# Layer 0 of a four-layer convolution stack: the last 1x1 convolution ordered by channel groups in place of chunks

## The chip, the core and the metric

The kernel runs on one core of one Trainium2 chip. Its engines work side by side, each through its own list of instructions in order: TensorE (PE; its weight loads are shown apart as PEld), VectorE (DVE), ScalarE (ACT), GpSimd (POOL) and SyncE (SP), which issues transfers. The metric is the device time of the whole kernel in microseconds (us), as the median of several runs.

## The reference, cut to what matters

The input x has 4 images of 64 channels and 256 x 256 pixels, all float32. Four residual layers follow one another. The change touches layer 0 alone, and in it the last line, the 1x1 convolution from 192 channels to 64, and the addition of x.

```python
def reference(x, L0_conv_w_in, L0_conv_w_dw, L0_conv_fft_filter, L0_conv_w_out, ...):
    # layer 0
    x = x + _L0_conv_ref(_gn(x), L0_conv_w_in, L0_conv_w_dw, L0_conv_fft_filter, L0_conv_w_out)
    # layers 1, 2 and 3 follow, each x = x + layer(_gn(x), ...); they are not touched
    ...
    return x

def _L0_conv_ref(x, w_in, w_dw, fft_filter, w_out):
    x = jnp.einsum('bchw,oc->bohw', x, w_in)                     # 64 -> 384 channels
    B, C, H, W = x.shape
    xp = x.reshape(B, C, H // 8, 8, W // 8, 8).transpose(0, 1, 2, 4, 3, 5)
    xf = jnp.fft.rfft2(xp) * fft_filter                          # a filter on 8x8 patches
    xp = jnp.fft.irfft2(xf, s=(8, 8))
    x = xp.transpose(0, 1, 2, 4, 3, 5).reshape(B, C, H, W)
    x = lax.conv_general_dilated(x, w_dw, ..., padding=[(1, 1), (1, 1)], feature_group_count=C)
    x1, x2 = jnp.split(x, 2, axis=1)
    x = jax.nn.gelu(x1, approximate=False) * x2                  # 192 channels
    return jnp.einsum('bchw,oc->bohw', x, w_out)                 # the last 1x1 conv: 192 -> 64
```

## The kernel before

Layer 0 works in 128 steps (4 images, 32 strips of 8 rows each); a loop turn `t` has several strips in hand at different stages: it transforms strip t+2, expands and inverts strip t+1, does the depthwise convolution of strip t, and the last 1x1 convolution (`project`) and the residual of strip t-1. Everything that TensorE writes goes to PSUM, in pairs of banks that are handed out in turn from four buffers:

```python
def pair(name):

    return pp.tile([128, 2, 512], F32, tag=f"p{next(turn) % 4}", name=name)

halves = [slice(0, C), slice(C, 128)]                                # C = 64
quarters = [slice(k * Q, (k + 1) * Q) for k in range(4)]             # Q = 32
```

So the fifth `pair` waits until whoever reads the first has done so. The 192 gated channels of a strip lie in two places. 128 of them are in `h` (partitions: 4 chunks j of two rows each, 32 channels in each; along the free axis 4 channel groups g). The other 64 are in `v` (partitions 0-63 hold the rows of chunks 0 and 1, partitions 64-127 those of chunks 2 and 3, for the gated part). `project(t, m)` does one half m, that is two of the four chunks, into one pair, and `add_residual(t, m)` adds that pair to x, which is in `r`:

```python
def project(t, m):

    chunks = [j for j in (2 * m, 2 * m + 1) if j in chunks_of(t)]
    if not chunks:
        return
    ps = po[t, m] = pair(f"pso_{t}_{m}")
    v, h = vt[t], ht[t]
    for j in chunks:
        for s in range(2):
            nc.tensor.matmul(
                ps[halves[s], j % 2, 0:W].rearrange("p (r w) -> p r w", r=2), woutc[halves[m]],
                v[halves[m], 2 * j : 2 * j + 2, s * HW2 : (s + 1) * HW2],
                start=True, stop=False, tile_position=(m * C, s * C),
            )
    for g in range(4):
        for j in chunks:
            for s in range(2):
                nc.tensor.matmul(
                    ps[halves[s], j % 2, 0:W].rearrange("p (r w) -> p r w", r=2),
                    wout[quarters[j], g, :], h[quarters[j], g, :, s * HW2 : (s + 1) * HW2],
                    start=False, stop=(g == 3), tile_position=(j * Q, s * C),
                )

def add_residual(t, m):
    if (t, m) not in po:
        return
    ps, r = po.pop((t, m)), rt[t]
    for b, row, lo, hi in rows_of(t):
        k = slice(max(lo, 2 * m), min(hi, 2 * m + 2))
        if k.start < k.stop:
            z = slice(k.start - 2 * m, k.stop - 2 * m)
            rk = r[:, k].rearrange("p k r w -> p k (r w)")
            nc.vector.tensor_add(rk, rk, ps[:, z, 0:W])
```

`tile_position` names the place in TensorE's 128 x 128 array that a matmul uses: 64 rows by 64 columns for `woutc` (its operands have 64 partitions each), 32 rows by 64 columns for `wout`. The profile shows each of these float32 matmuls as two LDWEIGHTS and two MATMUL instructions.

The other users of PSUM in a turn are, cut to their matmuls and to what frees the pair:

```python
def transform_x(t):                       # psF: 32 matmuls; ACT copies it to xf
    ...
    nc.scalar.copy(xf[t], ps)

def expand(t, g, k):                      # psu: 4 matmuls; DVE multiplies it by the filter
    ...
    nc.vector.tensor_mul(ups[t, g][:, :, k, :], ps[:, :, 0:384], flt.broadcast_to([128, 2, 384]))

def invert(t, g, i):                      # psy: 32 matmuls; ACT copies it to y, in two parts
    ...

def depthwise(t, i, *transfers):          # psd: 9 taps x 16 matmuls, in tiles of 32 x 32, two pairs
    ...
    tile_position=(q * Q, j * Q),

def vector_tap(t, k):                     # the taps of the third channel group, on DVE (tap 0 on ACT)
    ...
    nc.vector.scalar_tensor_tensor(v, s, wdw[:, 2, k : k + 1], v, ALU.mult, ALU.add)
```

A loop turn, in the order in which each engine gets its instructions (the order of the engines' lists is the order of the code):

```python
for t in range(NS + 2):
    ...
    vector_gelu(t - 1, 0)
    normalize_x(t + 2)
    vector_taps(t, 1)
    vector_gate(t - 1, 0)
    vector_gelu(t - 1, 1)
    vector_taps(t, 2)
    vector_gate(t - 1, 1)
    vector_taps(t, 3, 4)
    if t <= NS:
        loads = [(load_r, t, 0), (load_r, t, 1)]
        if exists(t + 3):
            loads += [(load_x, t + 3, 0), (load_x, t + 3, 1)]
        gate_part(t, depthwise(t, 0, *loads))
    next_stats(t - 1)
    next_norms()

    if exists(t + 2):
        transpose_x(t + 2)
    if exists(t + 1):
        invert(t + 1, 0, 0)
    if t - 1 in rt:
        project(t - 1, 0)
        add_residual(t - 1, 0)
    if exists(t + 2):
        transform_x(t + 2)
    if t - 1 in rt:
        project(t - 1, 1)
    vector_taps(t, 5)
    add_residual(t - 1, 1)
    if exists(t + 1):
        invert(t + 1, 0, 1)
        expand(t + 1, 1, 0)
        expand(t + 1, 1, 1)
        invert(t + 1, 0, 2)
        expand(t + 1, 1, 2)
        expand(t + 1, 1, 3)
    if t - 1 in rt:
        finish(t - 1)                     # statistics of the new rows, on DVE
    ...
    vector_taps(t, 6, 7)
    ...
        d = depthwise(t, 1, *moves)
        vector_taps(t, 8)
        value_part(t, d)                  # DVE multiplies h by psd
    ...                                   # invert(t+1, 1, 2), two expands, invert(t+1, 1, 0), tap 0 of t+1,
                                          # two expands, invert(t+1, 1, 1)
```

Of the kernel before, what the change touches and what calls it, by code (L numbers as in the profile page):

```python
# [17 lines left out]
C = 64  # L18
# [96 lines left out]
class _Net:  # L115
# [113 lines left out]
    def _layer0(self, ctx, dst):  # L229
        tc, nc, a, B, H, W = self.tc, self.nc, self.a, self.B, self.H, self.W  # L230
# [4 lines left out]
        def pair(name):  # L235

            return pp.tile([128, 2, 512], F32, tag=f"p{next(turn) % 4}", name=name)

        small = lambda name: pair(name)[:, 0, :]
        HW2 = W // 2  # L240
        NJ = H // 8
        NS = B * NJ
        Q = 32
        halves = [slice(0, C), slice(C, 128)]
# [11 lines left out]
        with tc.tile_pool(name="l0i", bufs=12) as p_i:  # L256
            bst0 = new_bst0(0)
            for k in range(NJ):
                t = p_i.tile([128, 4, W], F32, tag="st", name=f"st_{k}")
# [12 lines left out]
        ps = small("psf")  # L272
# [11 lines left out]
        woutc = cp.tile([128, C], F32, name="woutc")  # L284
# [14 lines left out]
        x0, xns, xT, xf, ups, yt, lt, vt, ht, rt, po, bst1, gt = ({} for _ in range(13))  # L299

        def load_x(t, *sides, ins=None):
            b, j = place(t)
            if t not in x0:
                x0[t] = p_x.tile([128, 8, HW2], F32, tag="x", name=f"x0_{t}")
            for s in sides:
                d = nc.sync.dma_start(
                    x0[t][halves[s]], a["x"][b, :, 8 * j : 8 * j + 8, s * HW2 : (s + 1) * HW2]
                )
                if ins:
                    self.after(d, ins)  # L310


        def rows_of(t):
            b, j = place(t)
            if j > 0:
                return [(b, 8 * j - 2, 0, 4)]
            parts = [(b - 1, H - 2, 0, 1)] if t > 0 else []
            return parts + ([(b, 0, 1, 4)] if t < NS else [])
# [13 lines left out]
        def normalize_x(t):  # L332
            if not exists(t):
                return

            xn = xns[t] = p_xn.tile([128, HW2 // 16, 2, 8, 8], F32, tag="xn", name=f"xn_{t}")
            self.normalize(
                xn.rearrange("p k n r w -> p r (k n) w"),
                x0.pop(t).rearrange("p r (m w) -> p r m w", w=8), 0, place(t)[0],
            )  # L340
# [33 lines left out]
        def new_y(t):  # L374

            ys = yt[t] = []
            for i in range(3):
                y = p_y.tile([128, 11, W + 2], F32, tag=f"y{i}", name=f"y{i}_{t}")
                nc.gpsimd.memset(y[:, :, 0 : W + 2 : W + 1], 0.0)  # L379
                if place(t)[1] == 0:  # L380
                    nc.gpsimd.memset(y[:, 0:3, 1 : W + 1], 0.0)
                ys.append(y)
# [35 lines left out]
        def chunks_of(t):  # L418
            return range(1) if t == NS else range(4)
# [66 lines left out]
                r = slice(4 * m, 4 * m + g.shape[1])  # L486
                nc.vector.tensor_mul(vt[t][halves[m], r], g[halves[1]], vt[t][halves[1], r])

        def project(t, m):

            chunks = [j for j in (2 * m, 2 * m + 1) if j in chunks_of(t)]
            if not chunks:
                return
            ps = po[t, m] = pair(f"pso_{t}_{m}")
            v, h = vt[t], ht[t]
            for j in chunks:
                for s in range(2):
                    nc.tensor.matmul(  # L498
                        ps[halves[s], j % 2, 0:W].rearrange("p (r w) -> p r w", r=2), woutc[halves[m]],
                        v[halves[m], 2 * j : 2 * j + 2, s * HW2 : (s + 1) * HW2],  # L500
                        start=True, stop=False, tile_position=(m * C, s * C),
                    )
            for g in range(4):
                for j in chunks:
                    for s in range(2):
                        nc.tensor.matmul(  # L506
                            ps[halves[s], j % 2, 0:W].rearrange("p (r w) -> p r w", r=2),
                            wout[quarters[j], g, :], h[quarters[j], g, :, s * HW2 : (s + 1) * HW2],
                            start=False, stop=(g == 3), tile_position=(j * Q, s * C),
                        )  # L510

        def add_residual(t, m):
            if (t, m) not in po:
                return
            ps, r = po.pop((t, m)), rt[t]
            for b, row, lo, hi in rows_of(t):
                k = slice(max(lo, 2 * m), min(hi, 2 * m + 2))
                if k.start < k.stop:
                    z = slice(k.start - 2 * m, k.stop - 2 * m)
                    rk = r[:, k].rearrange("p k r w -> p k (r w)")  # L520
                    nc.vector.tensor_add(rk, rk, ps[:, z, 0:W])  # L521

        def finish(t):
            r = rt[t]
# [67 lines left out]
        with ordered:  # L592

            for t in range(3):
                load_x(t, 0, 1)
            for t in range(2):
                normalize_x(t)
                transpose_x(t)
                transform_x(t)
            for k in range(4):  # L600
                expand(0, 0, k)
            new_y(0)
            for k in range(4):
                expand(0, 1, k)
                if k < 3:
                    invert(0, 0, k)
            for k in range(4):
                expand(1, 0, k)
                if k < 3:
                    invert(0, 1, k)  # L610
            vector_taps(0, 0)

            for t in range(NS + 2):

                if exists(t + 1):
                    new_y(t + 1)
# [19 lines that stand above are left out]
                    invert(t + 1, 0, 0)  # L638
                if t - 1 in rt:
                    project(t - 1, 0)  # L640
                    add_residual(t - 1, 0)
                if exists(t + 2):
                    transform_x(t + 2)
                if t - 1 in rt:
                    project(t - 1, 1)
                vector_taps(t, 5)
                add_residual(t - 1, 1)
                if exists(t + 1):
                    invert(t + 1, 0, 1)
                    expand(t + 1, 1, 0)  # L650
# [5 lines that stand above are left out]
                    finish(t - 1)  # L656
                next_norms()

                if exists(t + 1):
                    copy_y(t + 1)  # L660
                vector_taps(t, 6, 7)
                if t <= NS:
                    moves = [(store, t - 1, 0), (store, t - 1, 1), (load_stats, t, 0), (load_stats, t, 1)]
                    d = depthwise(t, 1, *moves)
                    vector_taps(t, 8)
                    value_part(t, d)
                else:
                    store(t - 1, 0, 1)
                next_norms()

                if t + 1 == NS or place(t + 1)[1] == 0:
                    last_y(t + 1)
                if exists(t + 1):
                    invert(t + 1, 1, 2)
                if exists(t + 2):
                    expand(t + 2, 0, 0)
                    expand(t + 2, 0, 1)
                if exists(t + 1):
                    invert(t + 1, 1, 0)
                vector_taps(t + 1, 0)  # L680
                if exists(t + 2):
                    expand(t + 2, 0, 2)
                    expand(t + 2, 0, 3)
                if exists(t + 1):
                    invert(t + 1, 1, 1)
                next_norms()
                for g in range(2):
                    ups.pop((t + 1, g), None)
                for done, k in ((vt, t - 1), (ht, t - 1), (rt, t - 1), (yt, t - 1), (lt, t - 1)):
                    done.pop(k, None)  # L690
            while norms:
                next_norms()
# [573 lines left out]
```

## Time and profile before

| what | before |
|---|---|
| time, median of 3 runs | 8142.03 us (8135.49 to 8143.44) |
| span of the profiled run | 8139.5 us |
| PE busy | 7787.5 us, 96% |
| DVE busy | 6201.2 us, 76% |
| ACT busy | 3597.8 us, 44% |
| POOL busy | 647.1 us, 8% |
| `project`, wout (L506), PE busy | 503.7 us, 8208 instructions, from 167.2 to 5130.1 us |
| residual addition (L521), DVE busy | 176.1 us, 260 instructions |

The profile is of one execution. A line such as L506 is a line of the kernel before. A group of instructions has its busy time (the union of its instructions), the mean length of one, and the idle time of its engine just before them with whoever ended it. The chain of waits is followed back from the last instruction and tells, for each piece of time, which engine and line everything else hung on. Layer 0 ends at about 5130 us, the other layers take the rest.

### The profile page before, as it was taken

How to read it: one execution, taken by the hardware profiler on the slowest of the kernel's cores; microseconds unless marked ns; L12 is line 12 of the kernel's file. 1: busy time of each engine (PE TensorE's matmuls, PEld its weight loads, DVE VectorE, ACT ScalarE, POOL GpSimd, SP SyncE). 2: the span in 40 equal slices, each digit the busy share in tenths (PEclk: the TensorE clock that was granted, in tenths of full speed). 3: DMA queues.
4: the chain of work that ended last, by engine and by line, in shares of the span. 5: the costliest groups of instructions: out<-in, count | busy, mean ns of one | idle time of the engine just before them, and what ended most of it. 6: DMA issues, size and time to landing. Idle time of an engine off the chain costs nothing.

```text
span 8139.5 us, 402431 instructions
## 1 busy us (share of the span) xinstructions
PE 7787.5 (96%) x191350; PEld 4493.9 (55%) x191350; DVE 6201.2 (76%) x5653; ACT 3597.8 (44%) x3853; POOL 647.1 (8%) x1465
## 2 busy tenths in 40 slices
PE   5999999999999999999999999999998999998887
PEld 3666666666666666666666666333333444443365
DVE  6888888888888888888888888433336998886345
ACT  2444444444444444444444444111115787874111
POOL 0000000000000000000000000000001222221000
PEclk9999999999999999999999999999999999999955
DMA  5222222222222222222111111788885666667779
GB/s 117 58 58 62 59 61 55 55 57 59 60 56 56 57 59 58 58 55 49 42 46 46 43 44 41 187 215 212 222 212 140 176 179 173 172 178 222 257 283 389
DMA packets 520862, 942.83 MB, mean 116 GB/s; under 512 B 44996, under 2 KB 308116, under 8 KB 501812
## 3 DMA queue, kind: packets, MB, share of 16 engines
q1 hardware_dynamic: 438708, 648.59, 29.1%
q0 software_dynamic: 80512, 268.50, 12.0%
q8 instruction: 1500, 24.58, 1.3%
q14 instruction: 142, 1.16, 0.0%
HBM read 648.48 MB, written 268.44 MB: 113 GB/s over the span
## 4 chain that ended last, share of the span: by engine, by line
PE 92%; DMA 4%; DVE 2%; issue 1%; ACT 1%; SPq 0%; ACTq 0%; POOLq 0%; DVEq 0%; POOL 0%
PE psd L434 31%; PE ps L753 12%; PE psy L407 10%; PE psu L369 8%; PE one L936 7%; PE pso L506 6%; PE div L895 5%; DMA x<-x 3%; PE pso L498 3%; PE psF L356 2%; PE psa L1110 2%; PE psz L925 2%; PE psT L346 2%; DMA st<-in_x_dram 1%; PE zero L936 1%
## 5 line engine op out<-in xcount | busy, mean ns | idle before, releaser
L434 PE MATMUL psd<-y,diag 32*32 32x512 f32 x73296 | 2539.8, 597 | 11.3 <-issue 10.8
L472 DVE SCALAR_TENSOR_TENSOR v<-y,sb_w_dw,v 128x2048 f32<-128x2048 f32 x1024 | 2391.9, 2336 | 108.4 <-ACT v L470 86.7
L434 PEld LDWEIGHTS psd<-y,diag 32*32 32x32 f32 x73296 | 1516.7, 103 | 870.0 <-issue 350.5
L414 ACT COPY y<-psy 128x512 f32<-128x512 f32 x1536 | 913.9, 658 | 1782.3 <-PE psy L407 1780.3
L372 DVE TENSOR_TENSOR up<-psu,flt 128x768 f32<-128x768 f32 x1024 | 932.0, 952 | 252.9 <-PE psu L369 252.6
L407 PEld LDWEIGHTS psy<-sb_c_bdft,up 64*64 64x64 f32 x49152 | 834.4, 135 | 335.3 <-issue 170.2
L753 PE MATMUL ps<-xn,wk 64*64 64x512 f32 x9216 | 1003.0, 592 | 9.6 <-ACT xn L210 9.6
L407 PE MATMUL psy<-sb_c_bdft,up 64*64 64x64 f32 x49152 | 901.4, 220 | 14.6 <-issue 13.0
L210 ACT ACTIVATE xn<-x,nb,r 128x1024 f32<-128x1024 f32 (+3 forms) x272 | 487.8, 1796 | 897.6 <-POOL xn L735 810.1
L369 PE MATMUL psu<-win,xf 64*64 64x384 f32 x8192 | 765.1, 485 | 10.5 <-DVE h L454 10.5
L753 PEld LDWEIGHTS ps<-xn,wk 64*64 64x64 f32 x9216 | 340.3, 134 | 664.0 <-issue 663.9
L759 DVE TENSOR_TENSOR xr<-xr,ps 128x512 f32<-128x512 f32 x256 | 173.7, 679 | 658.1 <-PE ps L753 658.1
L881 DVE TENSOR_TENSOR q<-xn 128x2313 f32<-128x2313 f32 (+2 forms) x256 | 627.4, 2494 | 13.1 <-ACT xn L210 13.1
L936 PE MATMUL one<-z,wp 32*32 32x512 f32 x16384 | 593.5, 596 | 15.0 <-issue 13.7
L882 ACT ACTIVATE q<-q 128x2313 f32<-128x2313 f32 (+2 forms) x256 | 528.8, 2085 | 30.0 <-DVE q L881 28.7
L506 PE MATMUL pso<-h,wout 32*64 32x256 f32 x8208 | 503.7, 381 | 0.0
L936 PEld LDWEIGHTS one<-z,wp 32*32 32x32 f32 x16384 | 371.6, 103 | 217.4 <-issue 81.0
L448 ACT ACTIVATE h<-psd 128x1024 f32<-128x1024 f32 x258 | 251.0, 1023 | 530.5 <-PE psd L434 530.5
L895 PE MATMUL div<-q,ones 64*32 64x512 f32 x8192 | 459.5, 593 | 11.6 <-ACT q L882 9.6
L379 POOL MEMSET y<- 128x22 f32 x384 | 52.2, 137 | 4494.6 <-ACT y L387 3478.6
L506 PEld LDWEIGHTS pso<-h,wout 32*64 32x64 f32 x8208 | 287.6, 131 | 197.9 <-issue 99.6
L521 DVE TENSOR_TENSOR r<-r,pso 128x512 f32<-128x512 f32 (+1 forms) x260 | 176.1, 678 | 266.8 <-PE pso L506 266.8
(121 smaller groups left out, 6861.7 us busy)
## 6 DMA issues: line engine op xcount, KB each, us to landing
x<-x SPq DMA_DIRECT2D x240, 640.0 KB, 7.5
x<-x SPq DMA_DIRECT2D x61, 2048.0 KB, 13.5
st<-in_x_dram SPq DMA_DIRECT2D x256, 256.0 KB, 3.6
x<-in_x_dram SPq DMA_DIRECT2D x256, 256.0 KB, 3.8
xr<-x SPq DMA_DIRECT2D x128, 512.0 KB, 5.3
x<-xr POOLq DMA_DIRECT2D x128, 512.0 KB, 6.3
r<-x SPq DMA_DIRECT2D x512, 128.0 KB, 4.1
x<-r POOLq DMA_DIRECT2D x512, 128.0 KB, 3.9
```

The lines of the kernel that those rows point to most:

```text
L369: nc.tensor.matmul(ps[halves[n], s, 0:384], xf[t][halves[s], n, 4 * g + k], win[halves[s]], start=True, stop=True)
L372: nc.vector.tensor_mul(ups[t, g][:, :, k, :], ps[:, :, 0:384], flt.broadcast_to([128, 2, 384]))
L407: nc.tensor.matmul(ps[halves[c], n, s, :, k, :], up[halves[n], s, k, i * 128 + c * C : i * 128 + (c + 1) * C], bdft[halves[n]], start=True ...
L414: nc.scalar.copy(yt[t][i][:, 3:11, w0 : w0 + 64].rearrange("p r (k n w) -> p n r k w", k=4, n=2), ps[:, :, s])
L434: ins = nc.tensor.matmul(d[q // 2][quarters[j], q % 2], diag[quarters[q], i, k, :], rows_in(t, i, quarters[q], j, dy)[:, :, dx : dx + W], ...
L472: nc.vector.scalar_tensor_tensor(v, s, wdw[:, 2, k : k + 1], v, ALU.mult, ALU.add)
L506: nc.tensor.matmul(ps[halves[s], j % 2, 0:W].rearrange("p (r w) -> p r w", r=2), wout[quarters[j], g, :], h[quarters[j], g, :, s * HW2 : ( ...
L753: nc.tensor.matmul(ps[s][halves[j]], wk[halves[s], k, :], xn[halves[s], r : r + 2, dx : dx + W], start=(k == 0), stop=(k == 8),)
L881: nc.vector.tensor_sub(d, p0, p1)
L882: nc.scalar.activation(d, d, AF.Square)
L895: ins = nc.tensor.matmul(ps[quarters[j], h], ones[halves[h]], q[n, g, k][halves[h], r + 2 * j : r + 2 * j + 2, o : o + W], start=(m == 0), ...
L936: ins = nc.tensor.matmul(rows2(ps[g])[quarters[j], k], w[quarters[i]], z[quarters[i], h, 2 * j + dy : 2 * j + dy + 2, dx : dx + W], tile_p ...
```

## The change

`project` is no longer split by chunks (m) but by channel groups. The first call does the `v` part (`woutc`) and channel group 0 of `h`, the second does groups 1, 2 and 3; both calls go over all four chunks. So matmuls that follow one another lie in four row groups of 32 in place of two (`wout`), and in two row groups of 64 in place of one (`woutc`). Both pairs of PSUM are taken in the first call, and both are complete only after the second, so the two residual additions stand together, behind tap 5. The number of matmuls, their shapes and the DVE instructions are the same. It is meant to use more of the array at a time.

```diff
--- before.py
+++ after.py
@@ -486,39 +486,41 @@
                 r = slice(4 * m, 4 * m + g.shape[1])
                 nc.vector.tensor_mul(vt[t][halves[m], r], g[halves[1]], vt[t][halves[1], r])
 
-        def project(t, m):
-
-            chunks = [j for j in (2 * m, 2 * m + 1) if j in chunks_of(t)]
-            if not chunks:
-                return
-            ps = po[t, m] = pair(f"pso_{t}_{m}")
-            v, h = vt[t], ht[t]
-            for j in chunks:
-                for s in range(2):
-                    nc.tensor.matmul(
-                        ps[halves[s], j % 2, 0:W].rearrange("p (r w) -> p r w", r=2), woutc[halves[m]],
-                        v[halves[m], 2 * j : 2 * j + 2, s * HW2 : (s + 1) * HW2],
-                        start=True, stop=False, tile_position=(m * C, s * C),
-                    )
-            for g in range(4):
-                for j in chunks:
+        def project(t, *groups):
+
+            if 0 in groups:
+                po[t] = [pair(f"pso_{t}_{m}") for m in range(1 if t == NS else 2)]
+                v = vt[t]
+                for z in range(2):
+                    for m in range(2):
+                        j = 2 * m + z
+                        if j not in chunks_of(t):
+                            continue
+                        for s in range(2):
+                            nc.tensor.matmul(
+                                po[t][m][halves[s], z, 0:W].rearrange("p (r w) -> p r w", r=2), woutc[halves[m]],
+                                v[halves[m], 2 * j : 2 * j + 2, s * HW2 : (s + 1) * HW2],
+                                start=True, stop=False, tile_position=(m * C, s * C),
+                            )
+            h = ht[t]
+            for g in groups:
+                for j in chunks_of(t):
                     for s in range(2):
                         nc.tensor.matmul(
-                            ps[halves[s], j % 2, 0:W].rearrange("p (r w) -> p r w", r=2),
+                            po[t][j // 2][halves[s], j % 2, 0:W].rearrange("p (r w) -> p r w", r=2),
                             wout[quarters[j], g, :], h[quarters[j], g, :, s * HW2 : (s + 1) * HW2],
                             start=False, stop=(g == 3), tile_position=(j * Q, s * C),
                         )
 
-        def add_residual(t, m):
-            if (t, m) not in po:
-                return
-            ps, r = po.pop((t, m)), rt[t]
+        def add_residual(t):
+            ps, r = po.pop(t), rt[t]
             for b, row, lo, hi in rows_of(t):
-                k = slice(max(lo, 2 * m), min(hi, 2 * m + 2))
-                if k.start < k.stop:
-                    z = slice(k.start - 2 * m, k.stop - 2 * m)
-                    rk = r[:, k].rearrange("p k r w -> p k (r w)")
-                    nc.vector.tensor_add(rk, rk, ps[:, z, 0:W])
+                for m in range(2):
+                    k = slice(max(lo, 2 * m), min(hi, 2 * m + 2))
+                    if k.start < k.stop:
+                        z = slice(k.start - 2 * m, k.stop - 2 * m)
+                        rk = r[:, k].rearrange("p k r w -> p k (r w)")
+                        nc.vector.tensor_add(rk, rk, ps[m][:, z, 0:W])
 
         def finish(t):
             r = rt[t]
@@ -638,13 +640,13 @@
                     invert(t + 1, 0, 0)
                 if t - 1 in rt:
                     project(t - 1, 0)
-                    add_residual(t - 1, 0)
                 if exists(t + 2):
                     transform_x(t + 2)
                 if t - 1 in rt:
-                    project(t - 1, 1)
+                    project(t - 1, 1, 2, 3)
                 vector_taps(t, 5)
-                add_residual(t - 1, 1)
+                if t - 1 in rt:
+                    add_residual(t - 1)
                 if exists(t + 1):
                     invert(t + 1, 0, 1)
                     expand(t + 1, 1, 0)
```

## The prediction

> **What bounds the kernel now.** I read the page first, its chain of waits (part 4) and its groups (part 5); then the chain in order of time over one turn of layer 0's loop; then the timeline of the stretch that changes; then DVE's waits over ten turns.
>
> ```profile
> PE 92%; DMA 4%; DVE 2%; issue 1%; ACT 1%; SPq 0%; ACTq 0%; POOLq 0%; DVEq 0%; POOL 0%
> ...
> L506 PE MATMUL pso<-h,wout 32*64 32x256 f32 x8208 | 503.7, 381 | 0.0
> ```
>
> PE alone sets the end, and the group of `wout` had no idle time before it. One turn, from the depthwise convolution of strip t to the next one:
>
> ```profile
> 2005.23 1.02 PE psT L346 x8
> 2006.26 1.09 PE psy L407 x64
> 2007.35 0.85 PE pso L498 x8
> 2008.20 1.89 PE pso L506 x32
> 2010.09 1.09 PE psF L356 x64
> 2011.18 0.87 PE pso L498 x8
> 2012.05 1.89 PE pso L506 x32
> 2013.93 1.09 PE psy L407 x64
> 2015.02 1.29 PE psu L369 x16
> ...
> 2034.41 9.83 PE psd L434 x257
> ```
>
> The columns are start, length and what ran. The pieces join with no gap, all of them on PE: whatever shortens a piece here shortens the turn, until another engine is in the way. The next psT starts at 2044.23 in the same chain, so this turn took 39.0 us; layer 0 (pso from 167 to 5130 us) averages (5130 - 167) / 128 = 38.8. The two calls of `project` are 2 x (0.86 + 1.89) = 5.5 us of it.
>
> What DVE does in that stretch (one turn later), and what it lacks:
>
> ```profile
> 2046.76 1.28 DVE L253 BATCH_NORM_STATS2 bst<-st 128x6 f32<-128x512 f32 x2
> ...
> 2049.16 0.69 DVE L521 TENSOR_TENSOR r<-r,pso 128x512 f32<-128x512 f32 x1 [1.12 <-PE pso L506]
> 2049.76 2.35 DVE L472 SCALAR_TENSOR_TENSOR v<-y,sb_w_dw,v 128x2048 f32<-128x2048 f32 x1
> ...
> 2053.00 0.69 DVE L521 TENSOR_TENSOR r<-r,pso 128x512 f32<-128x512 f32 x1 [0.89 <-PE pso L506]
> ```
>
> ```profile
> DVE up L372 <- PE psu L369: 19.4, 32, 1.1
> DVE r L521 <- PE pso L506: 18.6, 20, 1.3
> DVE v L472 <- ACT v L470: 5.9, 9, 0.7
> ```
>
> The last view covers 2000 to 2389 us, ten turns. DVE was busy 341.3 us of the 387.7 in the ten turns from 2000, 34.1 a turn, and it waits about 1.9 us a turn for pso, 1.9 for psu and 0.6 for ACT. It is the next bound, 4.6 us behind PE.
>
> **What the Trainium skill says.** "TensorEngine Tiling (Array Packing)", Tiling Modes: the array splits into 4 independent tiles of 64 x 64 or 8 of 32 x 64, and a change of mode drains it. The trace agrees: sets of four `wout` matmuls start 0.216 us apart (from single starts in the trace), and from the last `woutc` set to the first `wout` set it is 0.305, so a switch costs some 0.1 us. The same page, Gotcha 1: different row tiles must not use one PSUM bank at the same time. The change keeps that: chunk j writes bank j % 2 of pair j // 2, four banks for four row groups; half m of `woutc` writes pair m. "TensorE: Matmul & The Clock Gate", Part 3: a matmul with 32 rows takes as long as one with 128, the gain being tiles side by side. The trace agrees in the pieces above: 32 `wout` instructions in 1.89 us is 0.059 each, while one streams for 0.216, so four ran at once. The same page, Part 1 (architectural detail), gives TensorE a queue of 64 instructions; I use it against the second rival.
>
> **The change, part by part.**
>
> *woutc.* Before, the four matmuls of a call have one row half and two column halves: two tiles at a time. 8 instructions take 0.85 us, that is 4 sets of two, 0.213 each. Two calls: 1.70 us. After, m alternates within z, so four tiles go together: 16 instructions in 4 sets, 0.85 us. Saved 0.85.
>
> *wout.* Before, 32 instructions go over four tiles: 8 sets of 0.216 = 1.73, and 1.89 - 1.73 = 0.16 us for the switch and the slower second set. Two calls: 3.78 us. After, g 0 has 16 instructions over eight tiles, 2 sets; g 1 to 3 have 48, 6 sets. 8 x 0.216 + 2 x 0.16 = 2.05 us. Saved 1.73. The switches stay four a turn (into and out of `wout`, twice). That eight tiles run side by side is shown in layer 2: L895, in tiles of 64 x 32, takes 459.5 us for 8192 instructions of 512 columns, 0.056 each or 0.449 per set of eight, hardly more than twice the 0.216 for 256 columns.
>
> So PE's work falls by 0.85 + 1.73 = **2.58 us a turn**, if nothing waits.
>
> *The buffers.* A turn still takes as many pairs, but in another order: pso0, pso1, psF, psy in place of pso0, psF, pso1, psy. Call the start of the turn's first depthwise convolution 0 (2034.34 in the timeline). `project` now needs both pairs of that convolution free at its start, 11.83; ACT's second GELU ends at 11.39 there: no wait. psF takes the pair of psT, which ACT has copied at 12.29, and starts at 13.4: no wait. psu of `expand(1, 0)` takes pso0's pair and `expand(1, 1)` pso1's: both wait for a residual addition on DVE.
>
> *The additions.* They wait for pso once in place of twice and stand behind tap 5. In the trace psu started at 19.50; 2.58 less is 16.92. DVE: say tap 1 starts d after 0. It started at 0.49 here, and the statistics ended at 13.70; DVE's pieces between them follow each other without a wait. Tap 5 takes 2.35 more, less an overlap of 0.08, and ends at 15.97 = d + 15.48. pso is complete at about 15.9. So the first addition ends at d + 15.48 + 0.03 + 0.69 = d + 16.20, and with 0.06 for the signal (the lag seen before an addition) psu can start at d + 16.26. It wants to at 16.92. The wait is d - 0.66 where d is over 0.66. The second addition ends 0.61 later, and the second psu wants its pair 0.65 later: the same condition. In nearly all of the 125 turns that I read, d lies between 0.3 and 1.03, with a median of 1.00, as tap 1 waits for tap 0 on ACT. The mean of d - 0.66, counted as 0 where negative, is **0.24 us**.
>
> After that DVE follows PE as before: both are earlier by the same amount, tap 8 ends about with the second depthwise convolution as it did, and nothing else changes place.
>
> *Sum.* 2.58 - 0.24 = 2.34 us a turn, times 128 = 300 us. 8142 - 300 = 7842. I take off a small part (13 us, 4%) since DVE, with 34.1 us of work in turns of about 36.5, has less slack in the longer turns (new image, uneven PE): **7855 us**.
>
> **The rivals.**
>
> *DVE takes over.* It has 34.1 us of work, 1.9 of waits for psu and 0.6 for ACT that the change leaves alone: 36.6 us a turn, a gain of 2.2, and 7861 us. It would go lower only if the waits grew with each other. For it: the wait for tap 0 is in most turns. Against a worse case: DVE's waits for pso are idle time that goes. If every turn lost 0.5 us more: 7920.
>
> *PE's front end is the bound.* Ten turns have 11,684 pairs of load and matmul in 387.7 us, 33 ns a pair, and the depthwise convolution alone runs at 9.68 us / 288 = 34 ns. If pairs could not come faster than that, packing would give nothing, as their number is the same: 8142. Against it: psy takes 64 pairs in 1.09 us, 17 ns each, of which a queue of 64 instructions can have held 32 pairs at most; the other 32 in 1.09 us is 34, so that alone does not decide. But near 5073 us two psy in a row, 139 pairs, start within 2.0 us; less 32 from the queue that is 107 pairs, 19 ns each. Eight tiles need 0.216 / 8 = 27 ns. The depthwise convolution has 16 tiles of four instructions, as many as the queue holds, which may be why it is slower.
>
> *Packing over four row groups works in part.* The 16 tiles of the depthwise convolution take 2539.8 / 73296 x 16 = 0.554 us for 512 columns, 0.277 for 256. With that, `wout` costs 8 x 0.06 = 0.5 us more a turn: 64 us, and 7906.
>
> **Range and chances.** The range goes from 7810 (no wait of psu at all, and a little shorter switches) to 7950 (half packing and DVE's waits together). All mechanisms but the front end leave over 163 us, the 2%. Chances: 0.94 faster by over 2%, 0.05 within, 0.01 slower.
>
> **What would show it right or wrong.** In the profile after: `woutc` one piece of 0.85 us with 16 instructions a turn, `wout` pieces of about 0.6 and 1.45; the turn about 36.4 us; DVE's waits for pso down from 1.9 us a turn to under 0.3; a new wait of psu for r, 0.2 to 0.4 us in most turns; PE busy down by some 300 us in layer 0 and unchanged elsewhere. A `wout` set of 0.28 us would show the third rival, psy and psu growing by what `wout` loses the second, and long waits of psu for r the first. I am wrong if eight tiles don't run side by side here, or if DVE's additions come over a microsecond late.

## The result and the profile after

The changed kernel takes 7909.86 us (median of 4 runs, 7902.17 to 7916.6) beside 8142.17 for the kernel before: a ratio of 0.9716, with a 95% interval of 0.9699 to 0.9733. It is faster by 2.8%, 232 us, where 287 were predicted. Later runs were made on other chips. Each ratio below is to the kernel before on the same chip, which took 8142, 8130, 8120 and 8101 us on the four of them.

The chain in order of time over the stretch that changed, of the kernel after (start, length, what ran, all in us):

```profile
2033.03 1.02 PE psT L346 x8
2034.05 1.09 PE psy L407 x64
2035.14 0.93 PE pso L500 x16
2036.07 0.62 PE pso L509 x16
2036.69 1.09 PE psF L356 x64
2037.78 1.48 PE pso L509 x48
2039.26 1.09 PE psy L407 x64
2040.35 1.29 PE psu L369 x16
2041.64 0.79 PE psy L407 x51
2042.44 0.16 issue
```

The packing is there as predicted: `woutc` (L500) is one piece of 0.93 us with 16 instructions, `wout` (L509) pieces of 0.62 and 1.48 us. The two calls of `project` take 3.0 us of PE in place of 5.5. New is the last line, a piece of time in which PE waited for nothing that the profile shows, in the middle of an inverse transform. The page of the kernel after has the same: issue is 2% of the chain, where it was 1%, and psy's idle time has grown. First the page of the kernel before, then that of the kernel after (behind the bar: busy time, mean ns of one, idle time just before them and who ended it):

```profile
L407 PE MATMUL psy<-sb_c_bdft,up 64*64 64x64 f32 x49152 | 901.4, 220 | 14.6 <-issue 13.0
```

```profile
PE 88%; DMA 4%; DVE 4%; issue 2%; ACT 1%; SPq 0%; DVEq 0%; ACTq 0%; POOLq 0%; POOL 0%
...
L407 PE MATMUL psy<-sb_c_bdft,up 64*64 64x64 f32 x49152 | 933.1, 221 | 36.5 <-issue 33.7
L369 PE MATMUL psu<-win,xf 64*64 64x384 f32 x8192 | 791.1, 487 | 20.5 <-DVE h L454 10.0
```

What ended DVE's idle time ahead of the residual addition, first in the kernel before (L521), then in the kernel after (L523), and who waited for it there (behind the name: us, times):

```profile
  PE pso L506: 266.8, 246
```

```profile
  PE pso L509: 62.1, 74
...
  PEld psu L369: 32.1, 84
  PE psu L369: 6.6, 7
```

DVE's wait for pso fell from 266.8 us to 62.1, or 0.49 a turn, where under 0.3 was predicted. The predicted wait of psu for the additions is there too: 32.1 + 6.6 = 38.7 us, 0.30 a turn. But 32.1 of it is idle time of the weight loads (PEld), and that need not delay PE: in the turn above the load at 2040.64 waited 0.31 us for an addition, and psu still took 1.29 us in the chain, as before. The matmuls themselves waited 6.6 us. PE's busy time fell from 7787.5 us to 7529.5, by 258 where some 300 were predicted.

The turns themselves, from the start times of PE's matmuls (124 turns each, means): 39.10 us before and 37.30 after, 1.80 less. Cut at the starts of psT, `woutc`, psF, psy, psu and the next depthwise convolution, and in us:

| stretch | before | after, median | after, mean |
|---|---|---|---|
| first call of project | 2.85 | 1.61 | 1.63 |
| psF and second call | 3.84 | 2.57 | 2.72 |
| psy behind it | 0.98 | 0.99 | 1.21 |
| psu, psy, psu to the depthwise convolution | 3.63 | 3.80 | 3.94 |

The rest of the turn stayed within 0.1 us. The medians of the first two rows are the packing, 1.24 + 1.27 = 2.51 us a turn. Beside that, about 0.7 us a turn is lost, where the prediction had 0.24.

### The profile page after: what moved, and what is told of

The parts are those of the page before. It is cut to its first block, busy times and chain, and to the rows that moved or that the text cites. A ratio compares the mean times of both kernels' runs of the same rounds, so it can differ in the third digit from the quotient of the medians.

```text
span 7914.8 us, 402431 instructions
## 1 busy us (share of the span) xinstructions
PE 7529.5 (95%) x191350; PEld 4403.3 (56%) x191350; DVE 6190.4 (78%) x5653; ACT 3598.1 (45%) x3853; POOL 644.5 (8%) x1465
## 3 DMA queue, kind: packets, MB, share of 16 engines
q8 instruction: 1500, 24.58, 1.4%
## 4 chain that ended last, share of the span: by engine, by line
PE 88%; DMA 4%; DVE 4%; issue 2%; ACT 1%; SPq 0%; DVEq 0%; ACTq 0%; POOLq 0%; POOL 0%
PE psd L434 30%; PE ps L755 13%; PE psy L407 10%; PE psu L369 8%; PE one L938 7%; PE div L897 5%; PE pso L509 3%; DMA x<-x 3%; PE psz L927 2%; PE psa L1112 2%; PE psF L356 2%; DVE v L472 2%; PE psT L346 2%; PE pso L500 1%; DMA st<-in_x_dram 1%
## 5 line engine op out<-in xcount | busy, mean ns | idle before, releaser
L407 PEld LDWEIGHTS psy<-sb_c_bdft,up 64*64 64x64 f32 x49152 | 861.3, 135 | 353.2 <-issue 141.9
L407 PE MATMUL psy<-sb_c_bdft,up 64*64 64x64 f32 x49152 | 933.1, 221 | 36.5 <-issue 33.7
L369 PE MATMUL psu<-win,xf 64*64 64x384 f32 x8192 | 791.1, 487 | 20.5 <-DVE h L454 10.0
L884 ACT ACTIVATE q<-q 128x2313 f32<-128x2313 f32 (+2 forms) x256 | 529.0, 2086 | 30.5 <-DVE q L883 29.1
L369 PEld LDWEIGHTS psu<-win,xf 64*64 64x64 f32 x8192 | 311.1, 134 | 184.0 <-issue 83.2
L971 POOL DMA_DIRECT2D x<-r x512 | 271.9, 538 | 978.9 <-DVE r L968 953.4
L897 PEld LDWEIGHTS div<-q,ones 64*32 64x32 f32 x8192 | 152.7, 107 | 314.1 <-issue 244.4
```

The source lines that it names most:

```text
L369: nc.tensor.matmul(ps[halves[n], s, 0:384], xf[t][halves[s], n, 4 * g + k], win[halves[s]], start=True, stop=True)
L407: nc.tensor.matmul(ps[halves[c], n, s, :, k, :], up[halves[n], s, k, i * 128 + c * C : i * 128 + (c + 1) * C], bdft[halves[n]], start=True ...
L884: nc.scalar.activation(d, d, AF.Square)
L897: ins = nc.tensor.matmul(ps[quarters[j], h], ones[halves[h]], q[n, g, k][halves[h], r + 2 * j : r + 2 * j + 2, o : o + W], start=(m == 0), ...
```

## The experiments

Theory **W**: the loss is the wait of psu for DVE's additions. Theory **F**: a large part is TensorE's instruction supply. F comes from the trace: every stop of over 0.33 us between the starts of two matmuls of one group (psy, psF or pso), from 170 to 4900 us, was set against its place in PE's list of instructions. A stop counts with its length less 0.06 us, the usual distance. In the kernel before there are 30, with 15.9 us, and in the kernel after 126, with 62.1 us. All 30, and 110 of the 126 with 56.4 us, are a multiple of 256 instructions apart (within 3). The other 16 are none: they are matmuls of the last strips of layer 0, from 4881 to 4900 us, and in the kernel before such ones lie at 5129 us, outside the stretch. The instruction queue of the page after:

```profile
q8 instruction: 1500, 24.58, 1.4%
```

That is 24.58 MB in 1500 packets, 16,384 bytes each. PE has 191,350 weight loads and as many matmuls, 382,700 instructions, which is 255 to a packet. The stops end 1.4 us (1.25 to 1.60 in 90% of those before) after such a packet has ended. The places 256 instructions apart are called block ends below.

### Statistics over fewer columns

```diff
-                nc.vector.bn_stats(bst[:, k * n + i, :], tf[:, i * 512 : (i + 1) * 512])
+                nc.vector.bn_stats(bst[:, k * n + i, :], tf[:, i * 512 : i * 512 + 64])   # images 1 to 3
```

> The changed kernel, but the input statistics of images 1 to 3 are taken over 64 of every 512 columns (so these statistics are left out in part), which takes about 1.1 us a turn off DVE ahead of the residual additions. The changed kernel has 7909.9 us; a turn became 1.80 us shorter where 2.34 was predicted. Theory W (the missing half microsecond is psu waiting for the additions on DVE, more than the 0.24 us that was predicted): the wait goes and about 0.5 us a turn comes back, 7840 to 7855. Theory F (a part of it is TensorE's instruction supply: stalls at every 256th instruction of its list, in stretches where 256 instructions are used up fast): only the recorded wait of psu for r, 38.7 us in all, can come back, and PE reaches the next stretch sooner: 7870 to 7895, with as many stalls without a releaser as in the changed kernel.

This kernel leaves out seven eighths of the columns of these statistics. Measured: 7877.62 us, ratio 0.9694 (0.9681 to 0.9707). The recorded wait of psu for the additions fell only from 38.7 to 25.4 us. The stops at block ends were 40.1 us, but that says nothing of DVE: the changed kernel itself had 37.3 in a later run. The 50 us and more of W didn't come. The changed kernel was not run on this chip. It had 0.9716 on one chip and 0.9686 on another, so between 0 and 18 us are left as the effect.

### Tap 0 early, twice

```diff
+                vector_taps(t + 1, 0)
                 if exists(t + 1):
                     invert(t + 1, 1, 0)
-                vector_taps(t + 1, 0)
```

> The changed kernel with all its work, but tap 0 of the next strip stands ahead of one inverse transform in ACT's list, so that DVE's tap 1 need not wait for it (0.65 us in most turns) and all of DVE's work up to the additions comes about 0.6 us earlier. Theory W: the wait of psu for the additions goes nearly, 0.5 us a turn: 7845 to 7860. Theory F: the recorded wait alone goes, 0.3 us a turn at most: 7870 to 7895. If the copy that is now behind tap 0 frees its pair too late, the first depthwise convolution starts later: 7910 or more.

Measured: 7884.99 us, ratio 0.9698 (0.9685 to 0.9711). Inconclusive by itself, for the same reason. So it was run again beside the changed kernel:

> The changed kernel itself, on the chip of the three runs below, as their base. On three chips the kernel before had 8142, 8130 and 8101 us, and the median time of one instruction packet was 1.13 us in the runs of the first two and 1.04 on the third. Theory F: the changed kernel hangs more on these packets than the kernel before, so its ratio is lower where they are faster: 0.968 to 0.970 on a chip with 1.04 us, 0.971 to 0.972 with 1.13. If the supply plays no part: 0.9716 on every chip.

> Tap 0 early, beside the changed kernel on one chip. The earlier runs on different chips put it 0.0018 (15 us) ahead. Theory W: 50 us or more ahead of the changed kernel. Theory F: 10 to 40 us ahead.

Measured on that chip: the changed kernel 7867.06 us, ratio 0.9686 (0.9673 to 0.9699); tap 0 early 7864.92, ratio 0.9682 (0.9669 to 0.9695). No gain that can be measured: less than either theory expected. DVE was earlier, as meant: tap 1 started 0.2 us after the depthwise convolution in place of 1.1. But the addition of this kernel now waits for TensorE instead:

```profile
  PE pso L509: 113.7, 118
...
  PEld psu L369: 28.3, 93
  PE psu L369: 2.2, 4
```

DVE waits 113.7 us for pso, and psu still 30.5 for the additions (45.8 in the changed kernel on this chip): they are late because `wout` ends late. W falls as the main cause. The changed kernel's two profiles agree with that: on this chip its recorded wait of psu was longer (45.8 us beside 38.7), but its stops at block ends were 72 with 37.3 us, in place of 110 with 56.4, and its ratio was lower by 0.0030, 24 us. That is the direction that F expects. Whether the packets, 1.09 us in the median beside 1.13, make the difference is not shown by two chips.

### wout in halves, in both kernels

The same columns stream in twice as many instructions:

```diff
             for g in groups:
-                for j in chunks_of(t):
-                    for s in range(2):
+                for r in range(2):
+                    for j in chunks_of(t):
+                        for s in range(2):
...
-                            wout[quarters[j], g, :], h[quarters[j], g, :, s * HW2 : (s + 1) * HW2],
+                                wout[quarters[j], g, :], h[quarters[j], g, r, s * HW2 : (s + 1) * HW2],
```

> The changed kernel with each wout matmul of 256 columns done as two of 128: the same streaming time, but 128 more TensorE instructions a turn in each kind (64 pairs of load and matmul become 128). Without theory F only what 8 tiles cost beyond streaming is added, at most 0.15 us a turn: 7910 to 7930. Theory F: in the stretch of psF and wout 256 instructions are now used up in about 2 us, where in the changed kernel it is about 2.6 us and in the kernel before 4.2 us, and a turn has 5% more instructions: 0.7 to 1.5 us a turn more, 8000 to 8100, all of it stalls without a releaser.

> The kernel before with each wout matmul of 256 columns done as two of 128: as many more instructions as in the run above, but where wout uses four tiles and takes 1.89 us a call. Without theory F: no more than 0.1 us a turn, 8142 to 8155. Theory F: 256 instructions there take about 3.6 us, so stalls are rarer than in the run above: 0 to 0.4 us a turn, 8142 to 8195. What tells is the difference to the run above: F expects halving to cost the changed kernel clearly more (0.5 us a turn or more) than this one.

Measured: the changed kernel with halves 8114.02 us, ratio 0.9979 (0.9969 to 0.9988), the kernel before with halves 8154.71, ratio 1.0032 (1.0020 to 1.0043). Halving costs the changed kernel 0.0263 to 0.0293, 214 to 238 us, by either of its own ratios (8114 is 14 us over F's range); it costs the kernel before 25 us. The chain of the kernel before with halves, then that of the changed kernel with halves:

```profile
2010.67 1.09 PE psF L356 x64
2011.76 0.87 PE pso L498 x8
2012.62 1.91 PE pso L507 x64
```

```profile
2038.40 1.09 PE psF L356 x64
2039.49 1.55 PE pso L510 x90
2041.04 0.66 issue
2041.70 0.43 PE pso L510 x4
2042.13 1.09 PE psy L407 x64
2043.22 1.29 PE psu L369 x16
2044.52 0.68 PE psy L407 x44
2045.20 0.34 issue
```

Before, 64 half instructions take 1.91 us, where 32 whole ones took 1.89: halving costs the array next to nothing. In the changed kernel too, sets of eight matmuls side by side start 0.109 us apart, half of 0.216, until PE stops in the midst of `wout`. There are 247 stops with 216.4 us in that kernel, all of them at block ends. That is 160 to 179 us more than in the two profiles of the changed kernel, most of what halving costs; in the kernel before they rose from 15.9 us only to 18.9.

Where two stops are just 256 instructions apart (99 times), 3.3 to 4.7 us lie between their ends, with a median of 3.84. The second chain shows such a pair: 4 + 64 + 16 + 44 = 128 matmuls, 256 instructions with their loads, and from 2041.70 to 2045.54 it is 3.84 us. So that is what the next 256 instructions took to come.

The traces hold a second test, which changes no kernel. The block ends fall at other places in each turn, so one stretch of the turn can be compared with and without one in it (mean us over the same 124 turns; in brackets the number of turns after):

| stretch | before: without, with | after: without, with |
|---|---|---|
| psF and second call | 3.843, 3.843 | 2.580 (18), 2.741 (106) |
| psy behind it | 0.982, 0.982 | 1.032 (64), 1.407 (60) |
| psu, psy, psu to the depthwise convolution | 3.626, 3.637 | 3.714 (33), 4.028 (91) |

In the kernel before a block end in these stretches costs at most 0.01 us, in the kernel after 0.16 to 0.38. With `wout` in halves, psy takes 0.99 us without and 2.45 with. F holds.

### One part alone: woutc

```diff
-            for g in groups:
-                for j in chunks_of(t):
+            m = groups[0]
+            for g in range(4):
+                for j in [j for j in (2 * m, 2 * m + 1) if j in chunks_of(t)]:
...
-                    project(t - 1, 1, 2, 3)
+                    project(t - 1, 1)
```

(and the addition of half m is back where it was)

> One part alone: woutc over all four chunks in the first call, in four tiles as in the changed kernel, but wout by chunk halves in four tiles as before, each half with its addition where it was before. The step of the prediction gives 0.85 us a turn, 109 us: 8033 beside 8142, ratio 0.987. Theory F expects nearly all of it (stretches with wout in four tiles use up 256 instructions slowly; no new wait for an addition): 0.986 to 0.989.

Measured: 7994.96 us beside 8101.26, ratio 0.9870 (0.9853 to 0.9886), 106 us: the whole of the predicted 0.85 us a turn. With `wout` in four tiles there are 18 stops, 11.6 us.

### The other part alone: wout

```diff
-                for z in range(2):
-                    for m in range(2):
+                for m in range(2):
+                    for z in range(2):
```

> The other part alone: all as in the changed kernel, but the woutc matmuls go two tiles at a time as before (m in the outer loop). The step gives 1.73 us a turn, 221 us, less what is lost: theory F says that the stalls come from psF, wout and the inverse transforms, all still dense, so most of the 0.5 us a turn that got lost in the changed kernel is lost here too, though 0.85 us more of woutc gives DVE and the instruction supply a little time: ratio 0.977 to 0.983. If the parts were independent and lost nothing together, e5 and this one would add up to the changed kernel.

Measured: 7846.83 us, ratio 0.9686 (0.9671 to 0.9700), the same as the changed kernel's second ratio. A miss: it didn't undo what it was to undo, so no run shows `wout` alone. Its chain has

```profile
2011.63 0.93 PE pso L500 x16
```

Four matmuls started within 0.033 us there, and one row half has only two tiles. So the second row half started 0.026 us after the first, although all eight instructions of the first stand ahead of it in the list. So the two halves were taken apart by something that stands between them:

```diff
-                for z in range(2):
-                    for m in range(2):
-                        j = 2 * m + z
+            m = 1 if groups else 0       # no groups: the first call, ahead of psF
+            for z in range(2):
+                j = 2 * m + z
```

> The kernel with wout in one visit and tap 0 early, but the two row halves of woutc stand apart, one ahead of psF and one behind it, so that they cannot run at the same time. (In the run that put m in the outer loop, the 16 woutc instructions stood together, and the trace shows the second row half starting while the first was still going: woutc still took 0.93 us a turn. It did not undo that part.) Here woutc takes 2 x 0.85 us, 0.85 more a turn, 109 us: 0.9664 becomes 0.980 if all of it counts. Theory F: PE's extra time is also time for instructions to arrive and for the additions, so a third or more of it comes back: 0.975 to 0.978.

It is built on the kernel with `wout` in one visit:

```diff
-            if 0 in groups:
+            if not groups:
...
-                    project(t - 1, 0)
+                    project(t - 1)
...
-                    project(t - 1, 1, 2, 3)
+                    project(t - 1, 0, 1, 2, 3)
```

(and tap 0 early)

> The kernel with tap 0 early (ratio 0.9698), and in it woutc alone in the first call and all four groups of wout in the second, behind psF: two changes of TensorE's tiling a turn in place of four. Each change costs about 0.1 us at its start and 0.05 in its second set, so PE has 0.2 to 0.3 us a turn less to do: ratio 0.966 if all of it counts. Theory F: 128 pairs of load and matmul now take about 3.0 us there, no less than before, so stalls should not grow; but DVE's additions, which come at the same time, are now waited for about 0.25 us more in part of the turns: 0.966 to 0.970.

> The kernel with wout in one visit and tap 0 early, beside the changed kernel on one chip, to see whether it beats it: 20 to 45 us ahead of the changed kernel, 10 to 25 ahead of tap 0 early alone.

Measured: one visit 7831.28 us beside 8101.26, ratio 0.9664 (0.9650 to 0.9679); again, beside the changed kernel, 7851.58 beside 8119.61, ratio 0.9672 (0.9659 to 0.9686); with the halves of `woutc` apart 7889.35 us, ratio 0.9712 (0.9699 to 0.9726). One visit had the lowest time on both chips, 15 us under the changed kernel on the chip of both, less than the 20 to 45 expected, and the intervals overlap. With the halves apart 38 us are lost, of the 109 that the slower `woutc` was expected to cost PE, and less than the 70 to 94 that F expected. The chains, of the halves apart and then of two turns of one visit:

```profile
2067.82 0.82 PE pso L500 x8
2068.64 1.91 PE pso L509 x64
2070.55 1.09 PE psy L407 x64
```

```profile
2014.88 1.91 PE pso L509 x64
...
2049.91 0.93 PE psF L356 x64
2050.84 2.38 PE pso L509 x64
2053.22 1.09 PE psy L407 x64
```

With a slow `woutc` in front, the 64 instructions of `wout` take 1.91 us. Right behind psF they take 1.91 in one of these turns and 2.38 in the other. Over all 128 turns of one visit they are longer by more than 0.3 us in 33, and in each of these a block end falls among them; with the halves apart that happens in no turn. Stops at block ends fall from 52.4 us to 18.0 where the halves are apart. What `woutc` saves is thus paid back in part within the same turn.

### The additions ahead of tap 5

```diff
-                vector_taps(t, 5)
                 if t - 1 in rt:
                     add_residual(t - 1)
+                vector_taps(t, 5)
```

> The changed kernel with the two residual additions ahead of tap 5 in DVE's list, in place of behind it. In the changed kernel the statistics end about 2.2 us before pso is complete; tap 5 fills that time. So DVE idles some 2.2 us here, does tap 5 after the additions, and all of its work up to the value part comes about 1.7 us later: PE waits for the value part. Ratio 0.983 to 0.990 (1 to 1.7 us a turn of the gain lost). If DVE's order didn't matter: 0.972 as in the changed kernel.

Measured: 7936.25 us, ratio 0.9796 (0.9781 to 0.9810). Some 0.008 to 0.011 of the gain is lost, 65 to 89 us; the expected range began higher. The timeline of DVE in this kernel:

```profile
2006.51 1.28 DVE L523 TENSOR_TENSOR r<-r,pso 128x512 f32<-128x512 f32 x2 [1.76 <-PE pso L509]
2007.71 2.35 DVE L472 SCALAR_TENSOR_TENSOR v<-y,sb_w_dw,v 128x2048 f32<-128x2048 f32 x1
2009.98 3.54 DVE L372 TENSOR_TENSOR up<-psu,flt 128x768 f32<-128x768 f32 x4
```

DVE idles 1.76 us for pso and then does four products in a row, late. In the ten turns from 2000 us psu (loads and matmuls) waits 12.9 us for DVE's products, where the changed kernel has no such wait. Of the two places tried, the one behind tap 5, which the change chose, is the better.

## Why the prediction was right, point by point

The time, 7910 us, lies in the predicted range of 7810 to 7950, 55 us over the 7855 that was named.

- **woutc, 0.85 us a turn.** Right: alone it gave 106 us of 109. Beside the packed `wout` in one visit it is worth less: taking it away there cost 38.
- **wout, 1.73 us a turn.** Right, by the trace: together 2.51 of 2.58 by the medians, in pieces of 0.62 and 1.48 us where 0.59 and 1.46 were worked out. The third rival, packing that works in part, is out: sets of eight start 0.216 us apart, and 0.109 in halves. (What the prediction takes from the Trainium skill, that 32 rows take as long as 128, stands in "TensorE: Matmul & The Clock Gate" in the section "Why this matters for your kernels", not in Part 3.)
- **The buffers and the new wait of psu for r, 0.24 us a turn.** Right in place, too large in size. Where no block end falls, psy takes 0.05 us more than before and the stretch behind it 0.09, so the additions can have cost PE about 0.14 a turn; the recorded 0.30 is for the most part idle time of the weight loads. The reason given, that tap 1 waits for tap 0, covers a third of the recorded wait: with tap 0 early 30.5 of 45.8 us stayed, and the time did not change. (The prediction also read d a little short: from the zero that its sum uses, the first depthwise matmul, the turns before have a median of 1.06 us, which gives a mean of 0.30.)
- **The sum, 2.34 us a turn.** It was 1.80. The mis-sized term is TensorE's instruction supply, which the sum has as nothing. By the table with and without block ends, and 0.03 us in 27 turns of the first call, it took (0.03 x 27 + 0.16 x 106 + 0.38 x 60 + 0.31 x 91) / 124 = 0.55 us a turn. The counted stops alone are 56.4 - 15.9 = 40.5 us, 0.32 a turn; shorter ones and those between groups are not in them. Without block ends the packing gave 1.22 + 1.26 = 2.48, and 2.48 - 0.14 - 0.55 = 1.79. That 2.48 - 0.14 is again 2.34 is luck in part: the packing gave 0.10 less than predicted, and the additions cost 0.10 less.
- **The front end as the bound.** This rival was dismissed too far. The prediction's evidence, 139 pairs within 2.0 us near 5073 us, shows how fast PE takes instructions that have arrived, and it was read just short of a stop of 1.14 us (shown below). It says nothing of how fast 256 more arrive: 3.3 to 4.7 us, or 26 to 37 ns for a pair of load and matmul. The turn's mean was 33 before, so the supply was close behind PE all along. The change puts psF, `wout` and psy close together: from the start of psF, 128 pairs are 64 of psF, 48 of `wout` and 16 of psy, 1.09 + 1.48 + 0.27 = 2.8 us. Before, they were 64 of psF, 8 of `woutc`, 32 of `wout` and 24 of psy, 1.09 + 0.87 + 1.89 + 0.41 = 4.3 us.
- **DVE takes over.** Seen in single turns, at little cost. DVE's share of the chain rose from 2% to 4%, and in the run with m outside, whose time is that of the changed kernel, the chain runs through ACT and DVE for 19 us of the turn from 2033 to 2053 us. But freeing DVE in two ways gave between nothing and 18 us.

The chain of the kernel before, where those 139 pairs stand:

```profile
5072.87 2.48 PE psy L407 x158
5075.35 1.14 issue
5076.50 0.74 PE psy L407 x31
```

"Runtime: NRT & Kernel Launch" in the Trainium skill, section Instruction fetch mechanics, says that each engine's instructions come in blocks of 16 KiB, 256 instructions, and that the cost of crossing a block's end is mostly hidden. The packets and the 256 agree with this case. The cost agrees for the kernel before, with 15.9 us in stops of over 0.33 us, and not for the others: 56.4 us in the changed kernel, 216.4 with `wout` in halves.

What sets the pace at which the packets come is open. A kernel that has fewer instructions in the same time was not tried, nor one with the block ends moved to other places of the turn.

## What to carry to other kernels

When matmuls are packed side by side, TensorE uses up its list faster: count the instructions of the densest stretch against what 256 of them take to arrive (3.3 to 4.7 us here), as well as the array's time. Here twice as many instructions, each half as long, cost 214 to 238 us in the dense kernel and 25 in the other. A wait that the profile names, as psu for the additions here, may itself come from a late producer; taking the named engine out of the way is the test.

## What the runs showed of the hardware that was not expected

- Where a stretch is dense, TensorE can stop at a block end, every 256 instructions: 110 stops of over 0.33 us in the changed kernel, and none elsewhere but in the last strips of layer 0. The stop ends 1.4 us after a packet of 16,384 bytes, which itself takes 1.1 us.
- Matmuls of different row halves need not start in list order: with eight instructions of one half in front, the other half started 0.026 us after the first, and all 16 took 0.93 us, as when they alternate.
- Twice as many matmuls of half the columns, in four tiles, took 1.91 us in place of 1.89: the array itself didn't mind the shorter instructions.
